# Products on constants in TensorE's waits at the end of the first heads block and behind its barrier

## The chip, the cores and the metric

The kernel runs on one core of a Trainium2 chip. Its metric is the device time of one launch in microseconds (us), the median of several runs. One more execution is taken with the hardware profiler; all times of instructions are from it, counted from the start of its span. In the tables PE is TensorE's matmul, PEld its weight load, DVE VectorE, ACT ScalarE, POOL GpSimd and SP SyncE.

## The reference, cut to what matters

A stream x of 32 sequences of 64 tokens, 128 wide (2048 tokens in all, 16 tiles of 128), goes through four blocks, each an attention to a context and a feed-forward part. This case concerns the second half:

```python
x = x + _L2_xattn_ref(_layernorm(x), ctx, ctx, ...)   # 16 heads of 8, causal mask
x = x + _L2_ffn_ref(_layernorm(x), W_in, b_in, W_out, b_out)
x = x + _L3_xattn_ref(_layernorm(x), ctx, ctx, ...)   # 16 heads of 8, +1 outside a band
x = x + _L3_ffn_ref(_layernorm(x), gate_w, weight)    # top 2 of 8 experts
...
def quantize_a16(x):                                   # inside _L2_ffn_ref
    amax = jnp.clip(jnp.max(jnp.abs(x)), 1e-08, None)  # over the whole tensor
    scale = 32767.0 / amax
    return jnp.clip(jnp.round(x * scale), -32768.0, 32767.0) / scale
...
hidden = gelu(quantize_a16(x) @ W_in_sim + b_in)
out = quantize_a16(hidden) @ W_out_sim + b_out
```

The maximum in `quantize_a16` is over all tokens. Nothing of the L2 feed-forward part can be rounded before the last tile of the L2 heads has been added to x and normed: a barrier. A second one stands between `hidden` and `out`.

## The kernel before, in words

Everything stays on the chip; x is held as four groups (`g`) of four tiles. PSUM is eight banks under tags: two for `s`, two for `t`, one each for `c1`, `c2`, `g` and `n`. `bank` hands out the banks of a tag in turn, so an instruction that writes a bank waits until the reader of its last content is done.

`heads_xattn` runs the heads of a block (`i` 0 is L2, 1 is L3). `interleave` steps three tiles at a time through `heads_tile`, one stage per step, and puts other work between them. The stages of a tile are: `kb` on POOL, the keys spread by a head mask (L1244); scores on PE, a bf16 product of the mask by the identity (L1257) and an f32 product (L1258), in two halves of eight heads in the two `s` banks; maximum (L1259) and difference (L1260, `e`) on DVE; exp on ACT (L1261); eight transposes on PE (L1268, tags `c1` and `c2`) and their copy `hpT` on ACT (L1269); 32 products with the values (L1275, tag `g`, 18 columns each); reciprocal `rs` and product `ho` on DVE (L1283, L1284). At the end of a group, and in the last group after tiles 1 and 3 (`LAST_ENDS`), `ho` is transposed (L204, called from `turned`), copied to `hoT` (L1298), multiplied by Wo (L1305) and added to x (L1306). In block L2, `after` is `l2_ffn_inputs`: layer norm moments on DVE, the reciprocal root `ln_rstd` on POOL (L161), the normed `l_xn` on DVE (L183) and its largest magnitude in `l2am` (L1396).

Then comes the barrier, in `l2_ffn_hidden`. `heads_keys` of block L3 for two groups is called ahead of it: four f32 products of 128x512 (L1134, tags `t` and `n` in turn, two matmul instructions each) and their copies `hk` with a bias on ACT (L1144). `global_amax` reduces `l2am` to `x_one` (L1329), turns it by a product with the identity (L1332, tag `g`) and reduces it again to `x_all` (L1334). POOL adds a bias to x per group (L1415), which for the last group waits until `l_xn` has been read from x, and then makes `kb` for the first tiles of L3 (L1244). `scales` is four tiny DVE instructions. `codes` rounds the normed x: a product with the scale (L1348) and a subtraction (L1349) per group. Per group there follow transposes (L204, tag `t`), a bf16 copy `xq_hi` on ACT (L1433), the rest `xq_lo` on DVE (L1434), eight bf16 products with W_in (L1439, tags `s` and `c`), and gelu on ACT (L1440, `l_h`). After the second barrier come the L2 outputs, the L3 heads with `l3_ffn` of finished groups between them (its products are issued by `mm3`, L236), and the output.

The order on each engine isn't that of the program text alone. The tile framework schedules the instructions by an estimate of their times and keeps dependencies; `in_turn` adds an order between two instructions without a wait. [...]

## Time and profile before

| what | value |
|---|---|
| median of 3 runs | 919.5 us (918.66 to 922.35) |
| the profiled execution | 919.86 us, of which the span is 918.1 us |
| PE busy | 826.0 us (90%), 5832 instructions |
| DVE busy | 747.6 us (81%) |
| ACT busy | 559.2 us (61%) |
| POOL busy | 327.2 us (36%) |
| mean granted clock of TensorE | 0.961 |
| last L1306 of the L2 heads | 730.23 us |
| L1332 of the first barrier | 734.46 us |
| first gelu (L1440) | 743.08 us |

The span runs from the first to the last instruction; the time of the execution holds 1.8 us more. A row of the timeline names start, duration, engine, line of the kernel, operation, output and inputs, shape, and in square brackets the idle time of the engine before it and what ended that. The granted clock is the share of full speed at which TensorE ran; the profiler records it as 1.0 or 0.5, and a stretch that holds both shows the mean. PE's rows overlap, because matmuls are pipelined: the distance between starts tells the rate, the duration of a row the delay until its result is there.

### The profile page before, as it was taken

How to read it: one execution, taken by the hardware profiler on the slowest of the kernel's cores; microseconds unless marked ns; L12 is line 12 of the kernel's file. 1: busy time of each engine (PE TensorE's matmuls, PEld its weight loads, DVE VectorE, ACT ScalarE, POOL GpSimd, SP SyncE). 2: the span in 40 equal slices, each digit the busy share in tenths (PEclk: the TensorE clock that was granted, in tenths of full speed). 3: DMA queues.
4: the chain of work that ended last, by engine and by line, in shares of the span. 5: the costliest groups of instructions: out<-in, count | busy, mean ns of one | idle time of the engine just before them, and what ended most of it. 6: DMA issues, size and time to landing. Idle time of an engine off the chain costs nothing.

```text
span 918.1 us, 15721 instructions
## 1 busy us (share of the span) xinstructions
PE 826.0 (90%) x5832; PEld 678.2 (74%) x5838; DVE 747.6 (81%) x1888; ACT 559.2 (61%) x1082; POOL 327.2 (36%) x300
## 2 busy tenths in 40 slices
PE   4978999999999998899899799997999878898995
PEld 3878999998998976688787688784766637566673
DVE  5889899699779867968678887788888688989877
ACT  3545676666667479686777777564545385445442
POOL 3744465254323323501140211014465212536342
PEclk9998999999999999999999999998999799999977
DMA  7320000000000000001000000000000000000000
GB/s 188 92 81 25 1 13 13 12 1 1 1 13 1 1 14 0 15 1 33 1 1 1 1 1 1 0 24 1 1 1 1 1 1 1 2 1 1 13 13 23
DMA packets 22669, 13.73 MB, mean 15 GB/s; under 512 B 3008, under 2 KB 21952, under 8 KB 22592
## 3 DMA queue, kind: packets, MB, share of 16 engines
q1 hardware_dynamic: 18320, 10.62, 4.2%
q10 hardware_dynamic: 4272, 2.10, 0.9%
q8 instruction: 46, 0.75, 0.3%
q14 instruction: 31, 0.25, 0.1%
HBM read 11.66 MB, written 1.05 MB: 14 GB/s over the span
## 4 chain that ended last, share of the span: by engine, by line
PE 50%; DVE 27%; ACT 14%; issue 3%; POOL 2%; DMA 2%; SPq 1%; DVEq 0%; ACTq 0%; POOLq 0%
PE c_ps L917 6%; PE g_ps L479 5%; PE s_ps L445 4%; PE s_ps L1258 4%; PE c_ps L236 4%; PE g_ps L236 3%; PE t_ps L465 2%; PE c_ps L1268 2%; PE g_ps L1275 2%; PE s_ps L236 2%; ACT L940 2%; PE t_ps L236 2%; DVE nm L1259 1%; ACT L935 1%; DVE mh_lo L894 1%
## 5 line engine op out<-in xcount | busy, mean ns | idle before, releaser
L461 POOL TENSOR_TENSOR e<-e,rs 128x512 f32<-128x512 f32 x64 | 66.0, 1043 | 98.2 <-DVE rs L460 58.3
L161 POOL TENSOR_TENSOR ln_rstd<-ln_rs,neghalf 128x4 f32<-128x4 f32 (+1 forms) x38 | 39.7, 1045 | 144.0 <-DVE ln_rs L169 138.0
L1244 POOL TENSOR_TENSOR kb<-hk,head 128x1024 f32<-128x1024 f32 x32 | 63.4, 1984 | 73.5 <-PE s_ps L1258 60.4
L445 PE MATMUL s_ps<-kvT,G 128*128 128x128 f32 x512 | 73.6, 283 | 1.5 <-DVE e L451 1.5
L1258 PE MATMUL s_ps<-kb,hq 128*128 128x512 f32 x128 | 67.0, 608 | 5.4 <-ACT hq L1227 5.2
L445 PEld LDWEIGHTS s_ps<-kvT,G 128*128 128x128 f32 x512 | 67.4, 197 | 5.7 <-DVE e L451 1.7
L917 PE MATMUL c_ps<-mh_hi,w2e_hi 128*128 128x512 f32 x160 | 62.2, 428 | 4.9 <-ACT be L935 2.7
L479 PE MATMUL g_ps<-N,Ct 128*128 128x128 f32 x512 | 61.7, 275 | 0.0
L479 PEld LDWEIGHTS g_ps<-N,Ct 128*128 128x128 f32 x512 | 60.2, 192 | 0.7
L1261 ACT ACTIVATE e<-e 128x1024 f32<-128x1024 f32 x32 | 34.0, 1061 | 41.0 <-DVE e L1260 38.4
L1259 DVE TENSOR_REDUCE nm<-s_ps 128x8 f32<-128x512 f32 x64 | 43.6, 681 | 15.3 <-PE s_ps L1258 15.2
L473 ACT COPY Ct<-c_ps 128x512 f32<-128x512 f32 x64 | 38.2, 596 | 28.8 <-PE c_ps L236 22.8
L469 DVE TENSOR_TENSOR pT_lo<-t_ps,pT_hi 128x512 fp32r<-128x512 f32 x64 | 43.3, 680 | 14.8 <-ACT pT_hi L468 12.5
L1269 ACT COPY hpT<-c_ps 128x512 f32<-128x512 f32 x64 | 35.1, 589 | 32.1 <-PE c_ps L1268 32.0
L917 PE MATMUL c_ps<-mh_hi,w2e_lo 128*128 128x512 f32 x160 | 51.9, 402 | 0.0
L1275 PEld LDWEIGHTS g_ps<-hv,hpT 128*64 128x64 f32 x1024 | 35.6, 146 | 20.0 <-issue 6.9
L894 DVE TENSOR_TENSOR mh_lo<-m,mh_hi 128x1024 fp32r<-128x1024 f32 x32 | 40.4, 1262 | 12.3 <-ACT mh_hi L893 11.5
L917 PE MATMUL c_ps<-mh_lo,w2e_hi 128*128 128x512 f32 x160 | 49.4, 405 | 0.5 <-DVE mh_lo L894 0.5
L452 ACT ACTIVATE e<-e 128x512 f32<-128x512 f32 x56 | 35.3, 638 | 23.9 <-DVE e L451 23.6
L468 ACT CAST pT_hi<-t_ps 128x512 fp32r<-128x512 f32 x64 | 37.7, 593 | 18.3 <-PE t_ps L465 11.8
L425 ACT COPY G<-g_ps 128x512 f32<-128x512 f32 x60 | 35.8, 597 | 21.4 <-PE g_ps L236 20.5
L447 DVE TENSOR_REDUCE nm<-s_ps 128x4 f32<-128x512 f32 x64 | 42.9, 679 | 4.5 <-PE s_ps L445 4.2
(519 smaller groups left out, 2665.7 us busy)
## 6 DMA issues: line engine op xcount, KB each, us to landing
kv_tok<-in_x ACTq DMA_DIRECT2D x8, 128.0 KB, 3.3
kv_tok<-in_ctx SPq DMA_DIRECT2D x8, 128.0 KB, 2.9
x<-in_x SPq DMA_DIRECT2D x4, 256.0 KB, 6.9
ctx<-in_ctx SPq DMA_DIRECT2D x4, 256.0 KB, 3.4
w2e_raw<-in_L_ffn_expert_w SPq DMA_DIRECT2D x1, 768.0 KB, 4.5
out<-x SPq DMA_DIRECT2D x3, 256.0 KB, 2.3
WkT<-in_L_xattn_WkT ACTq DMA_DIRECT2D x2, 256.0 KB, 5.4
WqT<-in_L_xattn_WqT SPq DMA_DIRECT2D x2, 256.0 KB, 7.2
```

What stands on the lines that cost most here:

```text
L236: step = K.nc.tensor.matmul(ps, w[a], x[b], start=start and i == 0, stop=stop and i == 2)
L445: nc.tensor.matmul(ps[:, j, :], G[:, bb, h : h + 2, :].rearrange("p h s -> p (h s)"), kvT[:, bb, :], start=True, stop=True)
L447: K.mark = nc.vector.tensor_reduce(nm, ps, AX.X, ALU.max, negate=True)
L461: nc.gpsimd.tensor_tensor(e, e, rs.unsqueeze(2).to_broadcast([P, 4, P]), ALU.mult)
L469: nc.vector.tensor_tensor(lo, ps, hi.bitcast(F32), ALU.subtract)
L479: nc.tensor.matmul(ps, Ct[:, h, :], C.N[:, h, :], start=(h == 0), stop=(h == 15))
L894: nc.vector.tensor_tensor(lo, m, hi.bitcast(F32), ALU.subtract)
L917: nc.tensor.matmul(ps, K.w2p[part][:, 2 * n + i, cols], x[:, i, :, :], start=first, stop=last)
L1244: step = nc.gpsimd.tensor_tensor(kb, K.hk[C.i][g][:, :, t, :].unsqueeze(2).to_broadcast(full), K.head.unsqueeze(1).unsqueeze(3).to_broadca ...
L1258: nc.tensor.matmul(ps, hq[:, half, t, :, :].rearrange("p b s -> p (b s)"), kb[:, half, :, :], start=False, stop=True)
L1259: nc.vector.tensor_reduce(nm[:, heads], ps, AX.X, ALU.max, negate=True)
L1275: nc.tensor.matmul(po[b * S : (b + 1) * S, j, :, :].rearrange("p r d -> p (r d)"), pT[:, j, b * S : (b + 1) * S], K.hv[g][:, 2 * t + b, C. ...
```

## The change

A helper issues bf16 products of the identity by a mask constant (values 0 and 1, 128x512) into an `s` bank that nobody reads, in a fixed order behind a given instruction. In the last group of the L2 heads, two stand behind the transposes of tile 2, four behind those of tile 3, and two behind the values of tile 3; twelve stand behind the product of the first `global_amax`. Block L3 (second row of `WARM`) and the second barrier get none. The computation and its results are the same.

```diff
+WARM = ((0, 0, 2, 4), (0, 0, 0, 0))
+WARM_END = 2
...
         for j in range(4):
             h = n * 8 + 2 * j
-            nc.tensor.transpose(ps[:, j, :], ..., K.ident)
+            turn = nc.tensor.transpose(ps[:, j, :], ..., K.ident)
         nc.scalar.copy(pT[:, n * 4 : n * 4 + 4, :], ps)
     yield
+    warm = WARM[C.i][t] if g == NG - 1 else 0
+    if warm:
+        keep_warm(K, bank(K, "s", [P, 512]), warm, turn)
     po = bank(K, AV[C.i][t % len(AV[C.i])], [P, 8, 2, 9])
...
-            nc.tensor.matmul(
+            values = nc.tensor.matmul(
...
     xg = K.x[g][:, tiles, :]
+    if warm and t == GT - 1:
+        keep_warm(K, bank(K, "s", [P, 512]), WARM_END, values)
     ps = turned(K, o[:, tiles, :], QN[C.i])
...
-def global_amax(K, pool, per_group, name):
+def global_amax(K, pool, per_group, name, warm=0):
...
-    nc.tensor.matmul(ps, one.to_broadcast([P, P]), K.ident, start=True, stop=True)
+    step = nc.tensor.matmul(ps, one.to_broadcast([P, P]), K.ident, start=True, stop=True)
+    if warm:
+        keep_warm(K, bank(K, "s", [P, 512]), warm, step)
...
+def keep_warm(K, ps, n, after=None):
+
+    cols = ps.shape[-1]
+    moving = K.masks[1].rearrange("p h k -> p (h k)") if len(K.masks[1].shape) == 3 else K.masks[1]
+    for _ in range(n):
+        step = K.nc.tensor.matmul(ps, K.identb, moving[:, :cols], start=True, stop=True)
+        if after is not None:
+            in_turn(K, [after, step])
+        after = step
+    return after
...
-    amax = global_amax(K, wp, K.l2am, "x")
+    amax = global_amax(K, wp, K.l2am, "x", 12)
```

In the order in which the changed kernel issues, the twenty products stand as described. Besides, the amax product (L1332) now comes behind the fourth key product instead of ahead of it. Near the end of the kernel, one triple of expert products (L236) stands ahead of six gate products instead of behind them, and about thirty small DVE instructions of that stretch stand in another order. ACT, POOL and SP issue the same instructions in the same order as before.

More of the change, by code (lines that the diff above doesn't have):

```diff
@@ L1267, in heads_tile @@
             h = n * 8 + 2 * j
-            nc.tensor.transpose(ps[:, j, :], e[:, h : h + 2, :].rearrange("p h k -> p (h k)"), K.ident)
+            turn = nc.tensor.transpose(ps[:, j, :], e[:, h : h + 2, :].rearrange("p h k -> p (h k)"), K.ident)
         nc.scalar.copy(pT[:, n * 4 : n * 4 + 4, :], ps)
     yield
+    warm = WARM[C.i][t] if g == NG - 1 else 0
+    if warm:
+        keep_warm(K, bank(K, "s", [P, 512]), warm, turn)
     po = bank(K, AV[C.i][t % len(AV[C.i])], [P, 8, 2, 9])
```

## Prediction

> **What bounds the kernel now.** I read the page first, then TensorE's clock at the heads' end, then the timelines there. On the page the chain that ended last is half TensorE, and the row of the granted clock (tenths, 40 slices counted from 0) has dents at slices 3, 27, 31, 38 and 39.

> ```profile
> PEclk9998999999999999999999999998999799999977
> ...
> PE 50%; DVE 27%; ACT 14%; issue 3%; POOL 2%; DMA 2%; SPq 1%; DVEq 0%; ACTq 0%; POOLq 0%
> ```

> Slices are 22.95 us, so the dent at 31 (711.5 to 734.5 us) is the end of block L2's heads and what leads to the barrier. This stretch and the first L2 products, cut at the clock's steps (time; busy us and count of PE, PEld, DVE, ACT, POOL; clock; DMA):

> ```profile
> 716.00:723.50 7.50, 6.76 (x88) 4.78 (x87) 6.91 (x17) 3.54 (x5) 2.03 (x2) 1.00 0.01 2
> 723.50:733.80 10.30, 8.69 (x50) 5.76 (x49) 4.81 (x21) 2.64 (x6) 2.05 (x3) 0.50 0.00 0
> 733.80:740.60 6.80, 3.07 (x14) 1.60 (x13) 5.58 (x13) 4.63 (x10) 4.56 (x3) 1.00 0.01 4
> 740.60:744.00 3.40, 3.03 (x7) 1.25 (x8) 1.76 (x4) 1.51 (x4) 0.00 (x0) 0.50 0.00 0
> 744.00:768.00 24.00, 20.01 (x111) 12.59 (x109) 19.27 (x44) 23.40 (x39) 1.02 (x1) 1.00 0.00 1
> ```

> The clock is half for 10.2 us, whole for 6.8, half for 3.4: multiples of 3.4, so it is decided once per window of about 3.41 us, on boundaries 723.56, 726.97, 730.39, 733.80, 737.21, 740.62, 744.04. What decides is not PE's busy share: 720.15 to 723.56 is 2.67 us busy and loses the clock, 733.80 to 737.21 is 1.98 us busy and keeps it. It is nearer to the time in which columns stream. A 128x512 bf16 product lasts 0.38 us but the next starts 0.216 later (0.42 ns a column); an f32 one starts 0.43 later (0.84 ns); a transpose 0.11. The 32 value products of a tile have 18 columns each, so they stream 32 x 18 x 0.84 = 0.48 us of the 1.11 they last. Counted so, the window before the drop streams 1.4 us (values 0.48, four Wo products 0.44, five transposes 0.5): 0.41 of it. By the same count 508.5 to 511.9 has 0.38 and drops, 788.4 to 791.8 has 0.42 and stays, 733.80 to 737.21 has 0.57 and stays: the edge lies near 0.41. Back up it needs much more: 0.71 (887.4) stays at half, 0.85 (740.62) lifts.

> What half a clock costs, from PE's timeline (start, us, row, idle before):

> ```profile
> 721.11 1.11 PE L1275 MATMUL g_ps<-hv,hpT 128*64 128x18 f32 x32
> 722.15 0.71 PE L1305 MATMUL n_ps<-L_Wo,hoT 128*128 128x128 f32 x4
> 723.15 1.62 PE L1268 MATMUL c_ps<-ident,e 128*128 128x128 f32 x8 [0.29 <-ACT e L1261]
> ...
> 725.45 1.90 PE L1275 MATMUL g_ps<-hv,hpT 128*64 128x18 f32 x32 [0.46 <-ACT hpT L1269]
> ...
> 728.97 1.23 PE L1305 MATMUL n_ps<-L_Wo,hoT 128*128 128x128 f32 x4 [0.46 <-ACT hoT L1298]
> ...
> 739.42 1.09 PE L204 MATMUL t_ps<-ident,l_xn 128*128 128x128 f32 x8 [3.64 <-DVE l_xn L1349]
> ```

> Tile 2 (721.11) and tile 3 (725.45) do the same work at both clocks, one behind the other. PE then waits 3.64 us for the codes, and these wait for POOL:

> ```profile
> 733.16 1.26 POOL L1415 TENSOR_TENSOR x<-x,l_bo 128x512 f32<-128x512 f32 x1 [0.72 <-DVE l_xn L183]
> ...
> 734.67 3.94 POOL L1244 TENSOR_TENSOR kb<-hk,head 128x1024 f32<-128x1024 f32 x2 [0.25 <-ACT hk L1144]
> ...
> 735.87 3.03 DVE L1348 TENSOR_SCALAR l_xn<-l_xn,x_sc 128x512 f32<-128x512 f32 x2
> ```

> One by one, kb ends at 736.58 and 738.62, and the two L1348, 0.48 us each where POOL is idle, end at 736.86 and 738.90: each 0.28 behind a kb. So the barrier's end is set by kb; the amax, which made L1348 ready at 735.87, has 0.7 us to spare.

> **The change, step by step.** It removes nothing and adds 20 bf16 products (one load of 0.10 us and 0.216 of streaming each). In issue order they stand: 2 behind tile 2's transposes, 4 behind tile 3's, 2 behind tile 3's values, 12 behind the amax product. The amax product also falls behind the fourth key product, and near the kernel's end one triple of L236 passes six gate products, with DVE's order there. ACT, POOL and SP keep their order.

> 1. The two of tile 2. The first must wait until DVE has read its bank (e, 719.75 + 0.67 = 720.42); both are issued by 720.89. Behind them stands the transpose of ho, which started at 720.68: 0.2 late. It is covered: the values wait for hpT until 721.05 anyway, and Wo runs only at 722.15. Cost 0; uncovered 0.2.

> 2. Clock kept over tile 3. From the transposes' start to the values' start tile 2 needs 721.11 - 719.29 = 1.82, tile 3 needs 725.45 - 723.15 = 2.30: 0.48 to win. The four dummies stand in there: transposes issued by 723.15 + 0.87 = 724.02, dummies by 724.88, ho's transpose by 724.99, against hpT ready about 724.95. They cost 0.06; gain 0.42. Values to rs: 727.39 - 725.45 = 1.94 against 722.27 - 721.11 = 1.16, gain 0.78. The two dummies behind the values end near 726.5, before ho at 726.8: free. Transpose of ho to its copy: 0.51 against 0.36, gain 0.15. Wo to the sum in x: 1.26 against 0.75, gain 0.51. Together 1.86.

> 3. From x (L1306) to l_xn nothing changes (DVE and POOL). L1415, which waits for l_xn, moves from 733.16 to 731.3 and ends at 732.56; kb, which waited 0.25 more for hk, need not: at full clock a key product takes 0.86, so hk of the first keys is ready near 731.1. So kb starts near 732.6 instead of 734.67: **gain 2.1**. The amax: x_one at 731.87; the fourth key product needs hk's bank (731.10) and issues until 732.0; x_all about 732.55, L1348 ready 733.5, kb's first end 734.5. Its new place costs nothing; without that cover, up to 0.86.

> 4. The twelve dummies run 732.5 to 735.1 (12 x 0.216 = 2.6); the codes' first transposes come at 739.42 - 2.1 = 737.3. Spare 2.2 us at full clock; at half (5.1 us) 0.3 late.

> 5. The L2 products. Here eight ran at 0.43, and the first gelu began at 743.08. At full clock the last operand (xq_lo, 741.76) plus 0.4 gives 742.2: 0.9 more to win. But between the dummies' end and the transposes PE still idles 2.2 us. A window that starts within about 2.2 of its 3.41 us positions sees under 0.41 and drops the clock again. With the boundaries of this profile, 733.80 to 737.21 would stream 1.2 us (0.35): drop. I take 0 here; bounds 0.9 gain, and 0.5 loss if the drop catches the transposes too. From there ACT and DVE are back to back until the second barrier, so what is won stays won.

> 6. The end. A triple (0.7 us) ahead of the gate products delays their copy on DVE, which is full there, while W's halves come earlier: 0, bounds -0.7 and +0.7. The cold stretch at 884 to 894 shifts against the windows; one more or less of its three, from pairs of values at 1.9 against 1.1, is about 1.2 us either way.

> Sum: the profiled execution took 919.86 (span 918.1 and 1.8 around it); minus 2.1 is 917.8. It lies 0.36 over the median 919.5, so for a median I say **917.5**.

> [...]

> **Rivals.** (a) The clock is also kept over the products: 917.5 - 0.9 = 916.6. For it: about a third of the window positions. Against: the 2.2 us that PE still idles.

> (b) Slower: the dummies don't hold the clock (a product of constants by the identity counts less, or the edge lies above 0.54, what the window to 723.56 then streams), and stand at half speed ahead of tile 3's values. 724.56 + 4 x 0.427 + 0.2 = 726.5 instead of 725.45: 1.05 late; the two behind the values 0.15 more; L1415 then ends at 735.6 and kb starts 1.0 later: 920.5. It decides from the second cold dummy on (0.9 us lie between transposes and values). Against: the window at 740.62 was lifted by bf16 products alone.

> (c) The barrier is won but the end returns it (step 6, both against): 917.5 + 1.9 = 919.4. For it: DVE's order changes in the fullest stretch.

> (d) The end adds to it: 916.6 - 1.9 = 914.7.

> **Chances.** Forecast 0.50 (its own range 916.5 to 918.6), (a) 0.19, (b) 0.12, (c) 0.11, (d) 0.08. The range takes in (b) and most of (d): 914.9 to 921.0. Faster by over 0.5% (below 914.9, about what a measurement of this kernel can tell from no change) is (d) and a little of (a): 0.11. Slower by over 0.5% (above 924.1) needs (b) and (c) together and more: 0.03. Within: 0.86.

> **What would show it.** Right: clock 1.00 from 716 to past 733; the last values last 1.1; kb starts 2 us earlier; the transposes of the codes start near 737.3. Step 5: the clock 1.00 or 0.50 at the first L1439, and the first gelu at 741.0 or 740.1. Wrong: half clock before 733 with dummies in it (b); x two us earlier but kb not (another releaser); equal until 880 and then apart (c, d).

## The result, and the profile after

| what | before | after |
|---|---|---|
| median, 22 runs each | 919.63 us | 922.09 us |
| ratio after to before, 95% interval | | 1.0027 [1.0016, 1.0038] |
| the profiled execution | 919.86 us | 919.31 us |
| its span | 918.1 us | 917.6 us |
| mean granted clock | 0.961 | 0.962 |

The change made the kernel about 2.5 us slower, where about 2 us less had been forecast: 917.5 us was said, with a range of 914.9 to 921.0. One of the 22 executions after took 1160.5 us at a granted clock of 0.656; it is in the median, where it moves 0.1 us, and not in the ratio. The profiled execution after is the shortest of its runs (the others reach to 925.3), and so shows less than the whole loss. The row of the clock from the page after:

```profile
PEclk8999999999999999999999999998999999998887
```

The dent of the first heads' end, the 7 at slice 31 before, is gone. Two new dents stand at slices 36 and 37 (825.8 to 871.7 us, slices of 22.94 us counted from 0), where the row before was whole. Cut at its clock's steps, the profile after shows (time; busy us and count of PE, PEld, DVE, ACT, POOL; clock; DMA):

```profile
713.00:720.60 7.60, 7.28 (x88) 4.80 (x86) 6.66 (x18) 3.77 (x6) 2.28 (x2) 1.00 0.01 2
720.60:731.00 10.40, 9.39 (x67) 5.28 (x68) 5.87 (x26) 5.26 (x12) 3.43 (x4) 1.00 0.01 2
731.00:737.80 6.80, 4.39 (x24) 2.14 (x23) 6.77 (x13) 2.61 (x5) 3.14 (x2) 1.00 0.00 1
...
840.30:857.30 17.00, 15.62 (x48) 10.04 (x47) 9.46 (x25) 4.13 (x8) 4.42 (x4) 0.50 0.06 16
...
901.70:908.50 6.80, 6.80 (x19) 5.07 (x18) 4.17 (x26) 2.23 (x9) 0.00 (x0) 0.50 0.14 40
```

From 713 to 737.8 the clock is whole, as the change meant. But where the profile before had one half-clock stretch of 3.41 us, at 846.44, there is now one of 17.07 us from 840.29, with PE busy for 15.62 of 17.0 us; and the one near the end, 3.41 us long before, lasts 6.83.

Where the time went is read from the lead: for each row of DVE, ACT and POOL with the same name and number in both traces, its start before less its start after. The median lead is 1.8 us already at 100 us, long before the first added product: it arises between 47 and 60 us, where the profile of before has a half-clock stretch of 3.41 us at 51.13 and that of after has none. It is 2.43 at 700, 5.34 at 750, 5.36 at 815, 0.81 at 868 and 0.51 at the end. So this execution wins 2.9 us at the place of the change, loses 4.5 between 846 and 858 (in the times of the profile before), and loses 0.3 behind that.

### The profile page after: what moved, and what is told of

The parts are those of the page before. It is cut to its first block, busy times and chain, and to the rows that moved or that the text cites. A ratio compares the mean times of both kernels' runs of the same rounds, so it can differ in the third digit from the quotient of the medians.

```text
span 917.6 us, 15769 instructions
## 1 busy us (share of the span) xinstructions
PE 827.5 (90%) x5858; PEld 677.2 (74%) x5858; DVE 746.4 (81%) x1888; ACT 558.3 (61%) x1082; POOL 328.6 (36%) x300
## 3 DMA queue, kind: packets, MB, share of 16 engines
HBM read 11.66 MB, written 1.05 MB: 14 GB/s over the span
## 4 chain that ended last, share of the span: by engine, by line
PE 51%; DVE 26%; ACT 15%; issue 3%; POOL 2%; DMA 2%; SPq 0%; ACTq 0%; DVEq 0%; POOLq 0%
PE c_ps L917 6%; PE g_ps L479 5%; PE s_ps L1260 5%; PE s_ps L445 4%; PE c_ps L236 4%; PE g_ps L236 3%; PE c_ps L1270 2%; PE g_ps L1280 2%; PE t_ps L236 2%; PE t_ps L465 2%; PE s_ps L236 2%; ACT L940 2%; DVE mh_lo L894 1%; ACT L935 1%; DVE nm L447 1%
## 5 line engine op out<-in xcount | busy, mean ns | idle before, releaser
L1260 PE MATMUL s_ps<-kb,hq 128*128 128x512 f32 x128 | 69.2, 627 | 5.2 <-ACT hq L1229 5.2
L1261 DVE TENSOR_REDUCE nm<-s_ps 128x8 f32<-128x512 f32 x64 | 43.6, 681 | 18.4 <-PE s_ps L1260 18.0
L468 ACT CAST pT_hi<-t_ps 128x512 fp32r<-128x512 f32 x64 | 37.7, 592 | 16.8 <-PE t_ps L465 10.2
```

The source lines that it names most:

```text
L1260: nc.tensor.matmul(ps, hq[:, half, t, :, :].rearrange("p b s -> p (b s)"), kb[:, half, :, :], start=False, stop=True)
L1261: nc.vector.tensor_reduce(nm[:, heads], ps, AX.X, ALU.max, negate=True)
```

## The experiments

Three theories stood at the start. **T**: the new order of instructions at the end of the program costs the time. **W**: the barrier's time is won, and lost again where later work now lies differently to the windows in which the clock is decided. **S**: the added products don't hold the clock, or stand in the way. For longer rows of products, L says that each microsecond of delay costs one. All ratios are to the kernel before, measured together on one chip, with 95% intervals. "Old end" and "new end" mean the order of the last instructions of the kernel before and of the changed kernel; which of them a kernel gets comes out of the scheduler's estimate. VectorE's rows at the end stand in one and the same order in the four kernels with the new end (the changed one, bar14, heads_only, bar30), and as before in those with the old end (l3end: but for eight rows).

**1. bar16: sixteen products at the barrier, old end.**

```diff
-    amax = global_amax(K, wp, K.l2am, "x", 12)
+    amax = global_amax(K, wp, K.l2am, "x", 16)
```

> The change with 16 products behind the barrier's amax product instead of 12. The four more stand in TensorE's idle time (2.1 us there in the profile after), and with them the scheduler keeps DVE's and TensorE's order at the kernel's end as in the kernel before; the order at the heads' end and barrier is that of the change. Theory T (the loss comes from the new order at the end): the dummies' gain of 2.1 to 2.9 us stays and the loss goes, 917 us, ratio 0.997. Rival W (the loss comes from clock windows behind the barrier, whatever the order at the end): 922, ratio 1.003. Rival S (in most executions the dummies do not hold the clock and stand in the way): 921 to 922, and the profile shows half clock with dummies in it.

Measured: 0.9998 [0.998, 1.0015]. With four more products in the same wait, and the old end, the loss is gone, but no gain is seen: T's 0.997 and W's 1.003 both lie outside the interval.

**2. bar14: fourteen, new end.** The same line with 14.

> The same with 14 products; here the scheduler gives the order at the end of the changed kernel. Against the run with 16 it differs in two products that stand in idle time, and in the order at the end. Theory T: 922 us, ratio 1.003, 5 us more than the run with 16. Rivals W and S: also 922, but equal to the run with 16 within 1 us.

Measured: 1.0017 [0.9998, 1.0037]. With the new end a loss of about the same size is there again, though its interval just reaches to none.

**3. heads_only: none at the barrier, eight at the heads' end, new end.** The same line without its last argument.

> Only the eight products at the heads' end, none behind the barrier; order at the end as in the changed kernel. Theory T: gain 2.1 us less the loss of 5, so 922. Rival W: 920 to 922. Rival S: 921 to 922.

Measured: 1.003 [1.0015, 1.0045]. The products at the barrier are not what costs. In its profile the lead grows by 2.08 us between 700 and 750, which is the forecast's 2.1; with twelve to sixteen behind the amax product it grows by 2.89 to 2.92 in each of eight profiles.

**4. cols8: all twenty products, 8 columns wide instead of 512, old end.**

```diff
-    cols = ps.shape[-1]
+    cols = 8
...
-        step = K.nc.tensor.matmul(ps, K.identb, moving[:, :cols], start=True, stop=True)
+        step = K.nc.tensor.matmul(ps[:, :cols], K.identb, moving[:, :cols], start=True, stop=True)
```

> All twenty products, but each on 8 columns instead of 512 (streaming 3.4 ns instead of 216): they stand in the same places and cannot hold the clock. Order at the end as in the kernel before. Theory T: 919.6, as before, within 1 us; the clock falls at the heads' end as before. Rival W: as before too. Rival S (the places and waits of the products cost): 920.5 to 922.

Measured: 0.9998 [0.9981, 1.0015]. The clock falls at 724.04 for 10.24 us as before, and the lead changes by 0.03 us between 700 and 750. Places, waits and the moved amax product cost nothing that shows; what the products of 512 columns do, those of 8 in the same places do not. S is out.

**5 to 7. bar32, bar30, bar40: a row at the barrier longer than the wait.** The same line with 32 (old end), 30 (new end) and 40 (old end). Against bar16 the first L2 products come 1.8, 1.4 and 3.5 us later by the leads.

> 32 products behind the barrier's amax product, order at the end as in the kernel before: a clean delay. They run to about 737.0 where the codes of the run with 16 came at 734.9, so the first transposes and all behind them are 2.1 us later, with the clock held up to there. Theory W (what the heads' end wins is given back in clock windows further on, so the total hardly follows the work's place): within 1 us of the run with 16, 920.3. Rival L (linear: a delay ahead of the barrier's end is paid in full): 922.4.

> 30 products, 0.4 us less delay than with 32, but with the order at the end of the changed kernel. Theory T (that order costs by itself): 2 to 2.5 us over the run with 32 in spite of the smaller delay. Rival (the order is innocent, the difference between 14 and 16 was another): 0.4 us under it.

> 40 products, order at the end as before: the dummies end near 738.8, a delay of 3.9 us against the run with 16. Theory W: less than 2 us of the delay is paid, 920.5 to 922. Rival L: 924.2.

Measured: 0.9995 [0.9979, 1.0012], 1.0008 [0.999, 1.0027] and 1.0034 [1.0018, 1.0051]. A delay of 1.8 us at the barrier costs nothing that shows; one of 3.5 costs about 3. L's 922.4 for bar32, 1.002 of the kernel before, lies outside its interval. Since bar16's own time is no surer, 1.8 us is about the least that could be told here: that a microsecond at the barrier is not a microsecond at the end is likely, and not more. bar30, with the new end, stands 1.2 us over bar32; T had said 2 to 2.5 and its rival 0.4 under; the run lies between them and is too loose to decide. In the profile of bar40 the lead goes down by 4.67 us between 815 and 868, in that of bar32 by nothing.

**8. l3end: bar16, and eight products at the end of the L3 heads.**

```diff
-WARM = ((0, 0, 2, 4), (0, 0, 0, 0))
+WARM = ((0, 0, 2, 4), (0, 0, 2, 4))
```

> The change with 16 products at the barrier and eight more at the end of block L3's heads (2, 4 and 2, as at the end of L2's); DVE's order near the end differs from the kernel before in eight rows. Theory W: the half clock of 7 to 10 us near 884 goes, 2 us less than the run with 16, 918.3. Rival (TensorE is filled there by the expert products, and the dummies stand in their way): 920.5 to 922.

Measured: 1.0 [0.9981, 1.0019]. In its profile the stretch from 840.24 still lasts 17.07 us and that at 884 is as long as in bar16 (6.83 us): the place of these products is not where the clock is lost, and the 2 us that the expectation hoped for there do not come.

**9. mid4: bar16, and four products in the wait ahead of the long stretch.** What TensorE did there, from the timeline after (start, us, row, idle before):

```profile
836.90 0.64 PE L1280 MATMUL g_ps<-hv,hpT 128*64 128x18 f32 x14
837.48 0.66 PE L204 MATMUL n_ps<-ident,hqn 128*128 128x128 f32 x4
838.06 0.76 PE L1280 MATMUL g_ps<-hv,hpT 128*64 128x18 f32 x18
840.06 0.38 PE L1259 MATMUL s_ps<-outside,identb 128*128 128x512 bf16 x1 [1.24 <-DVE e L1262]
841.15 1.97 PE L1270 MATMUL c_ps<-ident,e 128*128 128x128 f32 x8 [0.71 <-ACT e L1263]
```

The window from 836.88 to 840.29 holds narrow products (18 columns) and 1.24 us of waiting: it streams about a third of its time by the count of the prediction, and the clock falls. Once at half, PE is slow enough to be busy for 2.7 to 3.4 us of each window, but four windows with transposes, gate products of 8 columns and waits do not lift it again; the fifth does.

```diff
+    if (C.i, g, t) == (1, 2, 1):
+        keep_warm(K, bank(K, "c1", [P, 512]), 4, values)
...
-    amax = global_amax(K, wp, K.l2am, "x", 12)
+    amax = global_amax(K, wp, K.l2am, "x", 16)
```

> The changed kernel with sixteen products behind the barrier's mean, and four more of the same kind behind the sums of one tile of the second layer's heads, at 838.2 to 840.2 us, where the profile of bar16 shows TensorE waiting 1.24 us for the next scores and where its clock fell at 840.53 for 17.07 us. Theory W (what the barrier won is given back where the work comes to lie differently to the clock's stretches): the stretch from 840.5 to 857.4 is gone from the profile, the rows keep their lead of 5.2 us at 858 and at least 3.5 of it at the end; profiled about 913 to 915, and 0.994 to 0.997 against the kernel before. Theory S (such products are in the way or hold nothing here): the clock falls at 840 to 847 all the same, ratio 0.9995 to 1.002. Theory C (whatever is won in one place is lost in the next weak one): the stretch is gone, but another of like length opens before 884, ratio 0.998 to 1.001.

Measured: 0.9958 [0.9941, 0.9974], faster than both kernels. The edit brings more than the four products: with them four transposes of `e` in each of two tiles come later in TensorE's order, and some thirty VectorE rows stand otherwise, around 841 to 850 us and at the end. mid_only has the same order. The same place in its profile:

```profile
840.15 0.76 PE L1280 MATMUL g_ps<-hv,hpT 128*64 128x18 f32 x18
840.84 1.04 PE L1374 MATMUL c_ps<-outside,identb 128*128 128x512 bf16 x4
842.62 0.38 PE L1259 MATMUL s_ps<-outside,identb 128*128 128x512 bf16 x1 [0.74 <-DVE e L1262]
843.70 0.66 PE L1270 MATMUL c_ps<-ident,e 128*128 128x128 f32 x4 [0.71 <-ACT e L1263]
```

And its stretch of 17.1 us behind the four products:

```profile
840.80:857.90 17.10, 14.99 (x104) 9.29 (x103) 13.87 (x41) 6.85 (x12) 6.19 (x6) 1.00 0.06 17
```

The wait is 0.74 instead of 1.24 us, the clock 1.00 instead of 0.50, and PE issues 104 products in the time in which the changed kernel issued 48 (this stretch begins 2 us earlier in the work, by the leads). No stretch of like length opens behind it, so C, as the expectation called it, is not seen. One thing weakens this profile: its windows lie at 840 us as in bar14, heads_only and bar32, which have no long stretch either without the four products. The profiles of mid_only and two_places lie there as the changed kernel's does, and they decide it.

**10. mid_only: the four products of mid4 alone.** No product at the first heads' end or the barrier.

```diff
-WARM = ((0, 0, 2, 4), (0, 0, 0, 0))
+WARM = ((0, 0, 0, 0), (0, 0, 0, 0))
...
-    amax = global_amax(K, wp, K.l2am, "x", 16)
+    amax = global_amax(K, wp, K.l2am, "x", 0)
```

> The kernel before, without any product on constants in the first heads' end or behind the barrier, with only the four behind the sums of that one tile of the second layer's heads (about 843.9 us there; TensorE waits 1.29 us from there). The kernel before loses only one stretch of 3.41 us here, at 846.44. Theory W: that one stretch goes or stays, worth 0 to 1.5 us: ratio 0.998 to 1.0, so that what bar16 with the same four has beyond it is the barrier's own gain, at least 2.5 us. Theory S: 1.0 to 1.002.

Measured: 0.9981 [0.9965, 0.9997]. Against it mid4 (917.14 to 918.58 us, measured together) gains 1.4 us by the medians, 2.1 by the ratios: that is what the products at the heads' end and barrier (24 here) are worth when the place at 840 is held in both. At least 2.5 had been expected.

**11. two_places: mid4, and eight products in the next weak wait**, behind the values of the second tile of the L3 heads.

```diff
+    if (C.i, g, t) == (1, 0, 1):
+        keep_warm(K, bank(K, "c1", [P, 512]), 8, values)
     if (C.i, g, t) == (1, 2, 1):
```

> As the kernel with sixteen products at the barrier and four in the second layer's third group, and with eight more behind the sums of the second tile of that layer's heads (786.8 to 788.7 us in the profile of mid4, where TensorE waits 1.83 us for the next scores, the clock's stretch streamed 0.39 and the clock fell at 789.90 for 3.41 us). Theory W: that stretch is gone, 1.7 us of lead more at 800; behind it the work lies 1.7 us earlier to the clock's stretches than in mid4, so that part or all of it can be lost again or something can be won: 0.992 to 0.997 against the kernel before, the likeliest 0.9945. Theory S (dummies in a wait this full delay the scores): the scores at 788.67 start over 0.2 us later, ratio 0.996 to 0.998.

Measured: 0.9955 [0.9938, 0.9973], 915.62 us, the profiled execution 913.74. From its timeline (which holds seven of the eight):

```profile
785.59 1.90 PE L1376 MATMUL c_ps<-outside,identb 128*128 128x512 bf16 x7
787.48 0.38 PE L1259 MATMUL s_ps<-outside,identb 128*128 128x512 bf16 x1
```

And at the place at 840:

```profile
837.26 0.76 PE L1280 MATMUL g_ps<-hv,hpT 128*64 128x18 f32 x18
837.95 1.04 PE L1376 MATMUL c_ps<-outside,identb 128*128 128x512 bf16 x4
839.74 0.38 PE L1259 MATMUL s_ps<-outside,identb 128*128 128x512 bf16 x1 [0.75 <-DVE e L1262]
```

A window ends here at 839.93, with a lead of 5.7: within half a microsecond of the work, that is where the edge at 840.29 with its 5.4 lies in the profile after. It holds the same narrow products and the same wait. The four products (0.86 us) bring what it streams from about 0.25 to 0.5 of its time, by the count of the prediction, and the clock does not fall: it stays whole from 632 to 877 us. Its profile keeps the 1.7 us that mid4's lost there. Over all runs the ratio is only 0.0003 below mid4's: what one execution loses at a place is not lost there in each.

**12. order_alone: the kernel before, with TensorE's new order at the end forced.** No products on constants.

```diff
-        mm3(K, ps[:, t, :], tokens(t), K.gate, True, True)
+        mm3(K, ps[:, t, :], tokens(t), K.gate, True, True, after=K.triple if (g, tiles.start, t) == (3, 0, 0) else None)
...
+            if (g, t, half) == (2, 3, 0):
+                K.triple = step
```

> The kernel before, without any product on constants; only the order at the end is forced to what the changed kernel has there on TensorE: one triple of the last gated layer ahead of the six gate products of the last group (the VectorE rows that follow from it stand otherwise than in either kernel, some thirty of them). Theory T (the order at the end costs by itself): 0.5 to 2 us, ratio 1.0005 to 1.002. If the order does nothing by itself and all of the loss is in the clock's stretches before it: 0.9990 to 1.0003.

Measured: 1.0002 [0.9985, 1.0019]. No cost of the triple by itself shows, though the interval does not exclude 1.7 us. Its profile told more than its time. Up to 880 us it is the kernel before, instruction for instruction, but its windows lie otherwise to the work: it has no half-clock stretch at 723, one of 6.83 us at 734.02, and the one of 17.07 us from 843.25, which the profile of before lacks. POOL's rows at the barrier, in order_alone (no product on constants):

```profile
729.17 1.27 POOL L1417 TENSOR_TENSOR x<-x,l_bo 128x512 f32<-128x512 f32 x1 [0.71 <-DVE l_xn L183]
730.39 3.94 POOL L1246 TENSOR_TENSOR kb<-hk,head 128x1024 f32<-128x1024 f32 x2
```

and in bar16 (twenty-four of them):

```profile
729.15 1.27 POOL L1436 TENSOR_TENSOR x<-x,l_bo 128x512 f32<-128x512 f32 x1 [0.72 <-DVE l_xn L183]
730.38 3.94 POOL L1246 TENSOR_TENSOR kb<-hk,head 128x1024 f32<-128x1024 f32 x2
```

At like leads at 700 (2.11 and 2.25), kb starts at the same time with the products and without: the 2.1 us that the prediction wanted to win there are in some executions not lost. What order_alone loses comes later, in the half-clock stretch at 734.02 (first gelu at 739.28, in bar16 at 737.93).

**13 and 14. The triple put back, and the triple put into bar16.** triple_back is the changed kernel (eight and twelve products, where the expectation says six and twelve) with an edge that holds the triple behind the gate products; bar16_triple is bar16 with the edge of order_alone.

```diff
+        if (g, tiles.start, t) == (3, 0, 1):
+            in_turn(K, [step, K.triple])
```

> The changed kernel (six and twelve products on constants as they were), with one edge of order added: the triple of the last gated layer that its order had moved ahead of six gate products stands behind them again, as in the kernel before; some forty VectorE rows of the end stand otherwise than in either kernel. If TensorE's order there is what costs (theory T): as bar16, 0.998 to 1.001 against the kernel before. If it is VectorE's rows or nothing of the end: 1.0015 to 1.003, as the changed kernel.

> The kernel with sixteen products at the barrier (0.9998 with the old order at the end), with the triple forced ahead of the six gate products as the changed kernel has it; VectorE's rows follow in a third order. Theory T with TensorE's order as the cause: 1.0015 to 1.003. If the triple alone does nothing, as order_alone without products on constants had it (1.0002): 0.9985 to 1.001.

Measured: 1.0007 [0.9991, 1.0022] and 0.9992 [0.9972, 1.0011]. In bar16 the triple does nothing, as in the kernel before. In the changed kernel taking it back leaves the time between the two forecasts, with an interval that holds both. So TensorE's triple by itself is not the cause of a loss of 2 us; the rest of the new end is VectorE's rows.

What the leads of the profiles say together (us of lead against the profile of before, at its 700, 750, 815, 868 us and at the end; "on" counts full-width products at heads and barrier):

| kernel | on | 700 | 750 | 815 | 868 | end | half-clock stretches between 700 and 880 |
|---|---|---|---|---|---|---|---|
| before | 0 | 0 | 0 | 0 | 0 | 0 | 723.6 (10.2), 740.6 (3.4), 846.4 (3.4) |
| cols8 | 0 | -0.5 | -0.6 | -0.6 | -0.5 | -0.5 | 724.0 (10.2), 741.1 (3.4), 846.9 (3.4) |
| order_alone | 0 | 2.1 | 3.8 | 2.5 | -2.1 | -0.2 | 734.0 (6.8), 788.6 (3.4), 843.2 (17.1) |
| mid_only | 0 | 2.2 | 3.9 | 2.6 | 3.1 | 2.9 | 734.0 (6.8), 788.6 (3.4) |
| after | 20 | 2.4 | 5.3 | 5.4 | 0.8 | 0.5 | 840.3 (17.1) |
| bar16 | 24 | 2.2 | 5.2 | 5.2 | 0.6 | 2.0 | 840.5 (17.1) |
| bar14 | 22 | 1.2 | 4.1 | -0.4 | -0.2 | -3.2 | 765.8 (3.4), 789.7 (6.8), 847.7 (3.4) |
| mid4 | 24 | 1.6 | 4.5 | 2.8 | 3.3 | 4.6 | 789.9 (3.4) |
| two_places | 24 | 2.8 | 5.7 | 5.7 | 6.2 | 6.1 | none before 877 |

## Why the prediction was wrong

**Steps 1 to 4 held.** The clock is whole through tile 3 (its values last 1.11 us at 722.71), the places cost nothing (cols8), PE's rows hold the twenty products in the order of issue (two from 718.04 us, four from 721.64, two from 723.75, twelve from 730.06), and the twelve end 2.13 us ahead of the codes' transposes, where 2.2 was said:

```profile
722.71 1.11 PE L1280 MATMUL g_ps<-hv,hpT 128*64 128x18 f32 x32
...
730.06 2.75 PE L1372 MATMUL s_ps<-outside,identb 128*128 128x512 bf16 x12
734.94 1.09 PE L204 MATMUL t_ps<-ident,l_xn 128*128 128x128 f32 x8 [2.13 <-DVE l_xn L1358]
```

kb starts at 730.19; with the lead of 2.43 that this execution had at 700 it is 732.62, and the prediction said 732.6. Against the profile of before the gain of step 3 was as forecast.

**Step 5 held better than forecast at its place.** The clock also stayed whole over the L2 products, here and in all eight profiles with twelve to sixteen products at the barrier, where the prediction gave this a third of the window positions. Its edge of 0.41 is not sharp even in its own profile: by its count the window from 699.66 streams under 0.4 and stays whole, and the one from 880.57 about 0.5 and loses the clock. The first gelu starts at 737.75, with the lead 740.18: rival (a)'s 740.1, so that 2.9 us are won there and not 2.1.

**What failed first: "so what is won stays won" (step 5).** The step looked only for waits of other engines between the barriers. It did not ask where the later work would come to lie to the clock's windows, though the prediction had found these windows, and step 6 asked it for one stretch only (884 to 894, about 1.2 us either way). Behind the second barrier there are waits that the profile of before passed narrowly: 788.4 to 791.8 streamed 0.42 and stayed whole, and at 846 one window fell and the next lifted it. Moved to other windows the same work loses 1.3 to 4.5 us between 750 and 815 (stretches at 765 and 790), or 4.6 at 846. The prediction's 0.42, read as proof of an edge, was also a warning.

**What failed second: the 2.1 of step 3 was the price of one execution.** The sum took 919.86 less 2.1 as if each execution had the stretches of the profiled one. order_alone and mid_only have no products there, the same code up to the barrier, and 1.7 us less stall between 700 and 750. All kernels with twelve to sixteen products at the barrier reach 2.9. The products are thus worth 2.9 us in executions that lie like the profile of before, and 1.2 in those like order_alone. The stretch at 846 goes with how the windows lie at 840 us, with products (after) and without (order_alone). The profile of before was poor at the barrier and lucky behind it. On the medians the products bring 1.4 to 2.1 us where the place at 840 is held (mid4 to mid_only), and no gain that shows in bar16, whose interval reaches from a gain of 1.8 us to a loss of 1.4. Whether the products make the long stretch more frequent is not shown: six of ten profiles with full-width products and without the four at 840 have it, and one of three without them.

**What failed third: step 6.** It took 0 for the new order at the end, with bounds of 0.7 either way. The kernels with the new end measure 1.0027, 1.0017, 1.003 and 1.0008, those with the old end 0.9998, 0.9998, 0.9995 and 1.0 (bar40, with its long delay, left out): 2.1 us between their means, by the single intervals give or take about 1. The profiles of after and bar16, alike until 868, part by 1.7 us from there to the end. From the timeline after:

```profile
899.49 0.33 PE L204 MATMUL g_ps<-ident,l_xn 128*128 128x128 f32 x1 [0.72 <-DVE l_xn L183]
...
901.08 0.27 PE L236 MATMUL n_ps<-gate_hi,l_xT_hi 128*128 128x8 f32 x1 [0.46 <-ACT l_xT_hi L1530]
...
902.68 0.77 PE L236 MATMUL s_ps<-W_hi,l_xT_lo 128*128 128x512 f32 x1
```

and from that of bar16:

```profile
898.74 0.33 PE L204 MATMUL g_ps<-ident,l_xn 128*128 128x128 f32 x1 [0.15 <-DVE l_xn L183]
...
900.33 0.27 PE L236 MATMUL n_ps<-gate_hi,l_xT_hi 128*128 128x8 f32 x1 [0.46 <-ACT l_xT_hi L1530]
...
901.83 0.66 PE L236 MATMUL s_ps<-W_hi,l_xT_lo 128*128 128x512 f32 x1
```

With the new end TensorE waits 0.72 us instead of 0.15 for the last normed tiles, since VectorE does other rows first. Counted with the leads at 868 (0.81 and 0.60) its transposes start 0.96 later. The six gate products, 8 columns wide, then fall behind the window's edge (901.73; in bar16 they are through by 901.97), the next window streams 0.7 to 0.8 of its time instead of over 0.9, and the clock is whole 3.41 us later. At half clock products of 128x512 started 0.43 us apart (from 741.55 in the profile of before), at full clock 0.216; by an estimate from these, one window more at half clock is half of 3.41, 1.7 us: all of the difference. The later start only brought the products behind the edge, and the position can do the same without it: l3end has the old wait of 0.15 us, its gate products run from 901.54 over an edge at 901.68, and this stretch is 6.83 us too. The other profiles agree. In six of sixteen (after, bar14, heads_only, bar30, l3end, triple_back) the last six gate products end 0.8 to 1.5 us behind the edge, and the stretch that starts there lasts 6.83 us; in the other ten they are through by the edge, in bar32 0.5 behind it, and it lasts 3.41. All four with the new end are among the six. They lose 0.3 to 3.0 us of lead from 868 us to the end; the six with the old end (before included, l3end among them) lie between a loss of 0.4 and a gain of 1.8. The step was mis-sized because it counted the triple's 0.7 us on TensorE and gave VectorE's thirty rows no price. That VectorE's rows are the cause is read from these profiles and from the runs with the triple: moved alone it leaves the stretch at 3.41 us, and put back it leaves the wait for the normed tiles at 0.73 us and the stretch at 6.83. A kernel with VectorE's new order alone was not run, so this part is argued and not shown.

**The rivals.** (a) was right at the barrier and wrong for the time. (c), the end returns what the barrier won, names a part that is real, but its 919.4 lacks the stretch at 846, which no rival held. (d), the end adds to the gain, is out by the same rows. (b) is out: no profile with full-width products shows half a clock while they run in the heads. The length of an idle gap does not tell by itself where the clock falls: in the profile after, the window ahead of 840.29 has no gap above 1.24 us and loses it, and the gap of 2.13 us ahead of 734.94 left it whole. What the prediction's sum passed over is that executions of one code differ: times of one kernel on one chip spread over 5 to 7 us (before, 917.08 to 923.87 in 23 runs), and a half-clock stretch at 49 to 52 us, where all kernels are still the same, stands in six of the sixteen profiles and not in the other ten. The whole effect here is 0.3 to 0.5%, and mid4 shows that it can be worked on.

What stays open is the closing of the sum: the end (about 2.1 us) and a barrier gain that bar16 does not show leave the 2.5 us lost explained within the intervals, not to the tenth.

## What to carry to other kernels

Where the steps of a profile's clock lie on one grid, as here at 3.41 us, the stall that it shows is that of one position of the work: take several profiles of the same code before a stretch of half clock is priced, and look for all places that stream just over the edge, since a gain ahead of them moves them. Fill the weak waits that lie in all executions (here the 18-column products and the wait of 1.24 us ahead of 840.29 are one), the late ones included, before a gain at an early one is counted. And if an added instruction changes the scheduler's estimate, the order that it changes elsewhere is part of the change; VectorE's rows ahead of a TensorE input want a price too.
